# A two-layer graph network on one core: the first layer's symmetric products by half, its matrix engine in program order, part of its weighting on GpSimd

## The chip, the cores and the metric

The kernel runs on one core of a Trainium2 chip. A core has TensorE (PE, which multiplies matrices and also transposes blocks, writing to PSUM), VectorE (DVE), ScalarE (ACT), GpSimd (POOL, which can't read PSUM) and the DMA queues that SP, ACT and POOL issue. Each engine works through its own queue in order and waits at semaphores. The metric is the device time of one execution in microseconds (us).

## What is computed

There are 16 batches (graphs) of 1024 nodes with 128 features, and a 1024 x 1024 weighted adjacency per batch whose pattern of non-zeros is symmetric while its weights are not. The first layer normalizes x and runs three convolutions one after the other:

```python
def _adapt_conv(h, edge_weight, W, b, is_last):
    h = h @ W + b
    nh = h / jnp.maximum(norm, EPS)          # norm of each row of h
    cos = jnp.einsum('bij,bkj->bik', nh, nh)
    ew = edge_weight * cos
    h = jnp.einsum('bpq,bqc->bpc', ew, h)
    # relu, except after the last
```

The matrix `cos` is symmetric; `edge_weight` (the adjacency) is not. The result is added to x. The second layer first thins out the adjacency's pattern ("dilation"): row by row, a row with more than ten neighbours loses about two of them, at even ranks, and what is removed in a row is removed in the mirrored column too, which later rows see. Then three graph convolutions on the thinned adjacency with batch normalization follow, a linear map, and a second residual sum. The dilation depends on the adjacency alone, not on the first layer.

## The kernel before

N = 1024 is cut into `NCH` = 8 blocks of P = 128. The program has three stages: the first layer together with the dilation; then, after a branch, the first graph convolution with the thinned adjacency (`masked`, `Sums`); then the other two (line 811 sums them) and the output.

**First layer** (lines 196 to 367). `order` lists the 48 convolutions, the layers of two batches alternating. `adjT_tile` (196) loads a column strip of the adjacency (`nat`), transposes its eight blocks on PE, copies them on ACT (line 145) to a tile of its own, and has POOL write it out for later stages (205). For a convolution, `features` (223) multiplies with the weights, `turned` (245) makes the transposed features `nhT`, `scaled` (251) the normalized ones `hS` (squares on ACT, one product on POOL, line 259). Eight steps q follow. `products(q)` (267) multiplies block row q of `nhT` with all of `nhT`, two pieces of 512 columns (line 274, PSUM tile `pg`), and DVE weights each piece straight from PSUM with the transposed adjacency into `ew` (line 277). `sums(q)` (280) adds `hS[q]` times `ew` into the PSUM tile `po` (line 286), `LAG` = 2 steps later. After the eighth, ACT copies `po` out (line 291). `residual` (296) transposes the result back and adds x, `next_layer` (312) normalizes for the second layer; both write out by POOL's queue. All f32 matmuls run as two passes each.

**Dilation** (lines 387 to 539). For each of eight row blocks k and each half of the batches (`BH` = 8 of them), `dilate` loads the adjacency rows (`an`) and, for k > 0, earlier decisions (`kl`, from DRAM, written by line 538), makes the 0/1 pattern on ACT (412, 413), transposes the earlier decisions on PE (`pk`, 421) and merges them on DVE (422). PE and ACT make a table T (437 to 448). Then `ROUNDS[k]` rounds of a fixed-point iteration follow: DVE compares (line 479, eight instructions of 128 columns in f16), PE counts removals (`pc`, 487), DVE subtracts (503). In the end, for every batch, DVE scans the pattern (530, 1024 columns), ACT takes a distance (531), DVE forms the keep mask (534, 537), and POOL writes it out (538).

**What sets the order.** Both parts are Python generators. `dilation()` yields weights; after each, `step0` (546) runs first-layer units until the first layer has got `SPREAD` = 0.96 times the same share of its units as the dilation has of its weights (lines 541 to 556). A unit is one step q with whatever is attached to it. The tile framework then schedules each engine's instructions by its own estimate of readiness, so an engine's order need not be the program's. PSUM tiles of the first layer come from `ps_sm`, `ps_g` and `ps_o`, those of the dilation from `ps_k`, two buffers each (`ps_o` one).

**Hand-over** (lines 559 to 590, 672). PE sums a vector of mishaps (`pf`), the value is loaded into registers, and a branch runs the dilation again in an exact form if it isn't zero. Then SP loads 17 pieces of weights, and `fetch(0)` loads the first batch's keep mask (`kb`) and normalized features for the second stage.

Of the kernel before, what the change touches and what calls it, by code (L numbers as in the profile page):

```python
# [16 lines left out]
P = 128  # L17
# [15 lines left out]
EW = 4  # L33

LAG = 2

LAG1 = 2

# [5 lines left out]
def tile_adj_preln_d2(  # L44
# [94 lines left out]
    def transposed(psum_pool, dst, src, nm, func=AF.Copy):  # L139

        for h in range(NHALF):
            pt = psum_pool.tile([P, CPH, P], F32, tag="sm", name=f"pt_{nm}_{h}")
            for c in range(CPH):
                nc.tensor.transpose(pt[:, c, :], src[:, h * CPH + c, :], ident)  # L144
            nc.scalar.activation(dst[:, h * CPH : (h + 1) * CPH, :], pt, func)  # L145


    with ExitStack() as actx:
# [3 lines left out]
        ps_g = actx.enter_context(tc.tile_pool(name="a_g", bufs=2, space=PSUM))  # L152
        ps_o = actx.enter_context(tc.tile_pool(name="a_o", bufs=1, space=PSUM))
        ps_k = actx.enter_context(tc.tile_pool(name="a_k", bufs=2, space=PSUM))
# [3 lines left out]
        for i in range(3):  # L158
            nc.sync.dma_start(w0[:, i, :], W[i])
            nc.sync.dma_start(b0[:, i, :], bW[i].partition_broadcast(P))  # L160
# [22 lines left out]
        nc.sync.dma_start(mi, nodemask.rearrange("b (c p) -> (b c) p", p=P))  # L183
# [12 lines left out]
        def adjT_tile(b, q):  # L196

            nat = pool2.tile([P, NCH, P], F32, tag="nat", name=f"nat_{b}_{q}")
# [3 lines left out]
            t = pool1.tile([P, NCH, P], F32, tag="adjT", bufs=2 * NCH + 1, name=f"adjT_{b}_{q}")  # L202
            transposed(ps_sm, t, nat, f"a{b}_{q}")
            t = t.rearrange("p c q -> p (c q)")
            nc.gpsimd.dma_start(adjT_d[b][q], t)
            return t

        class Batch:


            def __init__(self, b):
                self.b, self.l, self.aT, self.rn = b, 0, [], None

            def load(self):
                b = self.b
                xb = pool2.tile([P, NCH, D], F32, tag="xb", name=f"xb_{b}")
                nc.sync.dma_start(xb, x[b].rearrange("(c p) d -> p c d", p=P))
                h = pool2.tile([P, NCH, D], F32, tag="tt", name=f"h_{b}")
                layernorm_relu(pool2, h, xb, f"l0_{b}")
                self.hT = pool2.tile([P, NCH, P], F32, tag="hT", name=f"hT_{b}")  # L220
                transposed(ps_sm, self.hT, h, f"h{b}")

            def features(self, h):

                nm, l, rn = f"{self.b}_{self.l}", self.l, self.rn
                if h == 0:
                    self.hN = pool1.tile([P, NCH, D], F32, tag="hN", bufs=2, name=f"hN_{nm}")
                hc = slice(h * CPH, (h + 1) * CPH)
                pw = ps_sm.tile([P, CPH, P], F32, tag="sm", name=f"pw_{nm}_{h}")
                for c in range(CPH):  # L230
                    nc.tensor.matmul(
# [13 lines left out]
            def turned(self):  # L245

                nhT = pool1.tile([P, NCH, P], F32, tag="nhT", bufs=2, name=f"nhT_{self.b}_{self.l}")
                transposed(ps_sm, nhT, self.hN, f"n{self.b}_{self.l}")
# [18 lines left out]
            def products(self, q):  # L267

                nm = f"{self.b}_{self.l}_{q}"
                ew = pool2.tile([P, N], F32, tag="ew", bufs=EW, name=f"ew_{nm}")  # L270
                for h in range(NHALF):
                    pg = ps_g.tile([P, HALF], F32, tag="pg", name=f"pg_{nm}_{h}")
                    hs = slice(h * HALF, (h + 1) * HALF)
                    nc.tensor.matmul(  # L274
                        pg, lhsT=self.nhT[:, q * P : (q + 1) * P], rhs=self.nhT[:, hs], start=True, stop=True
                    )
                    nc.vector.tensor_tensor(ew[:, hs], pg, self.aT[q][:, hs], ALU.mult)  # L277
                return ew

            def sums(self, q, ew):  # L280
                nm = f"{self.b}_{self.l}"
                if q == 0:
                    self.po = ps_o.tile([P, N], F32, tag="po", name=f"po_{nm}")
                for h in range(NHALF):
# [603 lines left out]
```

## Time and profile before

| | |
|---|---|
| three runs | 3245.83, 3253.26, 3254.17 us; median 3253.26 |
| the profiled execution's own time | 3257.55 us |
| its span, first to last instruction | 3255.8 us, mean granted TensorE clock 0.963 |
| busy over the span | PE 2909.8 (89%), weight loads 2013.4 (62%), DVE 2131.6 (65%), ACT 1138.5 (35%), POOL 439.1 (13%) |
| first layer and dilation | 0 to about 1936 us |
| hand-over | about 1936 to 1977 us |
| second layer, first convolution | about 1977 to 2500 us |
| second layer, the rest | about 2500 to 3256 us |

How to read the profile: a row of a group names the line, the engine, the operation, what it writes and reads, the shape and the count; after the bar stand the busy time and the mean length of one instruction in ns, and after the second bar the time that the engine sat idle just before such instructions and what ended it. A timeline row has the start in us, the length, and the number of instructions merged into it. Matmuls are pipelined: the length of one overlaps the next, so the distance of starts tells the rate. A row that ends in "q" (SPq) belongs to an engine's sequencer, such as an issue of a DMA.

### The profile page before, as it was taken

The page shows a single profiled execution, that of the slowest core. Times are in us where ns is not written, and L with a number is a line of the kernel's source. Part 1 is how long each engine was busy: PE and PEld are TensorE (multiplying, and loading weights), DVE is VectorE, ACT ScalarE, POOL GpSimd, SP SyncE. Part 2 cuts the span into 40 slices and gives each one's busy share as a digit, 9 for nine tenths or more (in the row PEclk, how much of TensorE's full clock was granted, in tenths as well). Part 3 has the DMA queues.
Part 4 walks back from the last instruction along what each step waited for, and adds up shares of the span by engine and source line. Part 5 has one row for each costly group of instructions (what it writes and reads, how often), then busy time and mean ns, then how long its engine had stood idle before and what let it go on. Part 6 is the DMA issues. An engine that isn't in the chain of part 4 may idle for free. (4 is left out here: it accounts for less than half of the span.)

```text
span 3255.8 us, 45268 instructions
## 1 busy us (share of the span) xinstructions
PE 2909.8 (89%) x16547; PEld 2013.4 (62%) x16547; DVE 2131.6 (65%) x5319; ACT 1138.5 (35%) x2709; POOL 439.1 (13%) x539
## 2 busy tenths in 40 slices
PE   5999999899999999999999986888877999999996
PEld 4444445445454444445455436787766999889996
DVE  4668758868868768867877945666665333355555
ACT  6536445445345344345244211111111233222223
POOL 1111112012112012011111101111111000100000
PEclk9999999999999999999999998898988999999998
DMA  8337246246255264366175009999996666656663
GB/s 267 134 119 234 81 145 205 85 154 197 77 181 181 75 210 159 92 221 196 40 226 169 26 25 331 340 346 345 345 334 215 206 201 201 200 193 225 226 216 123
DMA packets 423271, 614.65 MB, mean 189 GB/s; under 512 B 80512, under 2 KB 296064, under 8 KB 423040
## 3 DMA queue, kind: packets, MB, share of 16 engines
q1 hardware_dynamic: 338048, 410.32, 39.7%
q0 software_dynamic: 51712, 184.58, 14.7%
q10 hardware_dynamic: 33280, 16.78, 1.8%
q8 instruction: 132, 2.16, 0.3%
q14 instruction: 99, 0.81, 0.1%
HBM read 418.65 MB, written 192.94 MB: 188 GB/s over the span
## 5 line engine op out<-in xcount | busy, mean ns | idle before, releaser
L274 PE MATMUL pg<-nhT 128*128 128x512 f32 x1536 | 771.9, 614 | 58.0 <-DVE ew L277 56.2
L286 PE MATMUL po<-ew,hS 128*128 128x512 f32 x1536 | 742.9, 601 | 3.1 <-POOL hS L259 2.6
L277 DVE TENSOR_TENSOR ew<-pg,adjT 128x512 f32<-128x512 f32 x768 | 516.4, 686 | 214.6 <-PE pg L274 205.8
L286 PEld LDWEIGHTS po<-ew,hS 128*128 128x128 f32 x1536 | 284.5, 192 | 318.2 <-issue 315.2
L811 PE MATMUL agg<-hw,aT 128*128 128x128 f32 x4096 | 472.0, 275 | 0.0
L811 PEld LDWEIGHTS agg<-hw,aT 128*128 128x128 f32 x4096 | 466.7, 192 | 4.0
L274 PEld LDWEIGHTS pg<-nhT 128*128 128x128 f32 x1536 | 263.8, 193 | 281.0 <-issue 151.1
L530 DVE TENSOR_TENSOR_SCAN rank<-patt 128x1024 f16<-128x1024 f16 x128 | 300.2, 2348 | 0.1
L710 PE MATMUL agg<-hw,aT 128*128 128x129 f32 x2048 | 263.5, 287 | 12.1 <-DVE aT L687 11.8
L710 PEld LDWEIGHTS agg<-hw,aT 128*128 128x128 f32 x2048 | 254.0, 202 | 19.4 <-DVE aT L687 12.5
L531 ACT ACTIVATE rank<-rank,fin 128x1024 f16<-128x1024 f16 x128 | 146.9, 1147 | 303.6 <-DVE rank L530 258.4
L687 DVE SCALAR_TENSOR_TENSOR aT<-raw,both 128x1024 f32<-128x1024 f32 x128 | 161.1, 1260 | 131.2 <-DMA raw<-adjT 129.5
L619 PE MATMUL pw<-wrx,hT 128*128 128x256 f32 x768 | 193.9, 404 | 10.4 <-ACT hT L764 9.7
L145 ACT ACTIVATE adjT<-pt_a 128x512 f32<-128x512 f32 x256 | 141.4, 591 | 164.7 <-PE pt_a L144 156.0
L621 DVE TENSOR_TENSOR own<-pw,bs 128x256 f32<-128x256 f32 x192 | 78.8, 422 | 182.3 <-ACT hw L620 182.3
L637 POOL TENSOR_TENSOR o<-o,rn_s 128x1024 f32<-128x1024 f32 x48 | 91.1, 1899 | 658.6 <-DVE rn_s L636 620.2
L620 ACT ACTIVATE hw<-pw 128x256 f32<-128x256 f32 x192 | 73.7, 384 | 301.8 <-PE pw L619 276.7
L619 PEld LDWEIGHTS pw<-wrx,hT 128*128 128x128 f32 x768 | 151.9, 204 | 34.9 <-ACT hT L764 10.5
L144 PEld LDWEIGHTS pt_a<-ident,nat 128*128 128x128 f32 x1024 | 123.2, 146 | 80.3 <-issue 48.1
L257 ACT ACTIVATE hS<-hN 128x128 f32<-128x128 f32 x384 | 113.7, 297 | 168.1 <-DVE hN L241 96.5
L144 PE MATMUL pt_a<-ident,nat 128*128 128x128 f32 x1024 | 149.6, 287 | 20.7 <-DMA nat<-in_adj_dram 10.5
L259 POOL TENSOR_TENSOR hS<-hN,rn 128x1024 f32<-128x1024 f32 x48 | 106.4, 2217 | 440.0 <-DVE rn L128 196.4
(154 smaller groups left out, 3550.9 us busy)
## 6 DMA issues: line engine op xcount, KB each, us to landing
aT<-adT SPq DMA_DIRECT2D x256, 512.0 KB, 4.3
an<-in_adj_dram SPq DMA_DIRECT2D x128, 512.0 KB, 4.8
nat<-in_adj_dram SPq DMA_DIRECT2D x128, 512.0 KB, 4.9
adjT<-adjT POOLq DMA_DIRECT2D x128, 512.0 KB, 5.1
raw<-adjT SPq DMA_DIRECT2D x128, 512.0 KB, 6.5
adT<-aT POOLq DMA_DIRECT2D x128, 512.0 KB, 7.1
keep<-kp POOLq DMA_DIRECT2D x128, 256.0 KB, 2.3
kb<-keep SPq DMA_DIRECT2D x128, 256.0 KB, 10.6
```

The costliest lines, as they stand in the source:

```text
L144: nc.tensor.transpose(pt[:, c, :], src[:, h * CPH + c, :], ident)
L145: nc.scalar.activation(dst[:, h * CPH : (h + 1) * CPH, :], pt, func)
L257: nc.scalar.activation(hS[:, c, :], self.hN[:, c, :], AF.Square, accum_out=ss[:, c : c + 1])
L274: nc.tensor.matmul(pg, lhsT=self.nhT[:, q * P : (q + 1) * P], rhs=self.nhT[:, hs], start=True, stop=True)
L277: nc.vector.tensor_tensor(ew[:, hs], pg, self.aT[q][:, hs], ALU.mult)
L286: nc.tensor.matmul(self.po[:, hs], lhsT=self.hS[:, q, :], rhs=ew[:, hs], start=q == 0, stop=q == NCH - 1)
L530: nc.vector.tensor_tensor_scan(rank, pt[:, 1 : N + 1], pt[:, 2:], 0.0, ALU.add, ALU.add)
L531: nc.scalar.activation(rank, rank, AF.Abs, bias=shift[:, i : i + 1])
L619: nc.tensor.matmul(pw[:, i, :], lhsT=hT[:, 2 * h + i, :], rhs=wrx[:, l, :], start=True, stop=True)
L687: nc.vector.scalar_tensor_tensor(aT, raw, 0.0, both, ALU.max, ALU.mult)
L710: nc.tensor.matmul(self.place(c), lhsT=aT[:, c * P : (c + 1) * P], rhs=self.hw[:, j, :], start=False, stop=j == NCH - 1 and (c % GA == GA ...
L811: nc.tensor.matmul(agg[:, c, :], lhsT=aT[:, c * P : (c + 1) * P], rhs=hw[:, j, :], start=False, stop=j == NCH - 1 and c % CPH == CPH - 1,)
```

## The change

`products` computes only the block columns from q to the end (36 of 64 blocks per convolution). ACT copies them from PSUM to an SBUF tile `g`; POOL multiplies `g` with the adjacency row into the first part of `ew`. `turn`, one step later, transposes the blocks of `g` right of the diagonal on PE into a PSUM tile of a new pool `ps_t`, and DVE weights these into the second part of `ew`. `sums`, three steps later (`LAG` = 3), adds the first part in pieces inside a PSUM bank; `sums_back` adds the mirrored blocks one by one into column block q of `po`, each with its own `hS` block as weights. The steps go through the block rows as `SEQ` says, a long row and a short one in turn. All matmuls and transposes of this stage are held in program order by `tc.keep_in_program_order`.

Beside that: the transposed adjacencies of two batches lie in one tile `adjA`, and strips (`adj_piece`) are loaded ahead and transposed at fixed places (`pieces`); x is kept in a tile of the batch (`fetch`), the first layer's norm is split off (`norm`, `enter`). The yields of the first layer carry PE's estimated time (`COLS` per block of a matmul, `TURN` per transpose), those of the dilation have other weights and more places. `rows` loads the dilation's rows one batch ahead. The dilation's PSUM tiles come from `ps_sm`; `ps_k` is gone. ACT copies `pe` to SBUF before DVE subtracts it. Counting on PE (`removed`) stands after the yield that follows DVE's comparisons. The first layer's weights are loaded by ACT's queue, the second layer's 17 pieces by POOL's, after `fetch(0)`. The last batch's `residual` and `next_layer` stand after the branch.

```diff
-EW = 4
-LAG = 2
+SEQ = (0, 7, 1, 6, 2, 5, 3, 4)
+LAG = 3
...
+COLS, TURN = 0.215, 0.109
...
+        def matmul(*args, **kwargs):
+            tc.keep_in_program_order(nc.tensor.matmul(*args, **kwargs))
...
+            def products(self, s):
+                q = SEQ[s]
+                row = NCH - q
...
+                most = max(NCH - c for c in SEQ[s % 2 :: 2])
+                g = pool1.tile([P, most, P], F32, tag=f"g{s % 2}", name=f"g_{nm}")
+                for c in range(0, row, CPH):
+                    n = min(CPH, row - c)
+                    pg = ps_g.tile([P, CPH, P], F32, tag="pg", name=f"pg_{nm}_{c}")
+                    matmul(
+                        pg[:, :n, :].rearrange("p c q -> p (c q)"),
+                        lhsT=self.nhT[:, q * P : (q + 1) * P],
+                        rhs=self.nhT[:, (q + c) * P : (q + c + n) * P],
+                        start=True,
+                        stop=True,
                     )
-                    nc.vector.tensor_tensor(ew[:, hs], pg, self.aT[q][:, hs], ALU.mult)
...
+                    nc.scalar.activation(g[:, c : c + n, :], pg[:, :n, :], AF.Copy)
+                nc.gpsimd.tensor_tensor(
+                    ew[:, :row, :],
+                    g[:, :row, :],
+                    self.aT[:, q, q * P :].rearrange("p (c q) -> p c q", q=P),
+                    ALU.mult,
+                )
+                return ew, g
...
+            def turn(self, s, ew, g):
...
+                for c in range(1, row, CPH):
+                    n = min(CPH, row - c)
+                    pt = ps_t.tile([P, CPH, P], F32, tag="gt", name=f"gt_{self.b}_{self.l}_{q}_{c}")
+                    for i in range(n):
+                        transpose(pt[:, i, :], g[:, c + i, :], ident)
+                    at = row + c - 1
+                    nc.vector.tensor_tensor(
+                        ew[:, at : at + n, :],
+                        pt[:, :n, :],
+                        self.aT[:, q + c : q + c + n, q * P : (q + 1) * P],
+                        ALU.mult,
                     )
...
+            def sums_back(self, s, ew):
...
+                for n in range(1, NCH - q):
+                    matmul(
+                        self.po[:, q * P : (q + 1) * P],
+                        lhsT=self.hS[:, q + n, :],
+                        rhs=ew[:, NCH - 1 - q + n, :],
...
+                    if now:
+                        behind.append((now, s, *now.products(s)))
+                        yield (NCH - q) * COLS
+                    late = None
+                    if len(behind) > LAG or not now:
+                        late, s_, ew, _ = behind.pop(0)
+                        late.sums(s_, ew)
+                        yield (NCH - SEQ[s_]) * COLS
+                    if s > 0 and now or s == 0 and i:
+                        b_, *of = behind[-2 if now else -1]
+                        if now or s == 0:
+                            b_.turn(*of)
+                            yield (NCH - 1 - SEQ[of[0]]) * TURN
+                    if late:
+                        late.sums_back(s_, ew)
+                        yield (NCH - 1 - SEQ[s_]) * COLS
...
-                yield 0.75
+                yield 3.0
...
-                    yield 0.1
+                    yield 2.5
...
-                    yield 0.1
+                    yield 1.0
...
-                    pc = removals(x, f"{nk}_{r}")
-                    yield 1.5
+                    removals(x, f"{nk}_{r}")
+                    yield 5.0
+                    pc = removed(f"{nk}_{r}")
                     x = pool2.tile([P, BH], F32, tag="x", name=f"x_{nk}_{r}")
                     nc.vector.tensor_tensor(x, x0, pc, ALU.subtract)
+                    yield 1.0
...
-                yield 2.5
+                yield 3.5
...
-                yield 1.3
+                yield 2.0
...
+        blocks = NCH * (NCH + 1) // 2
+        conv = (blocks + NCH * NCH + NCH) * COLS + (blocks - NCH + NCH + NCH) * TURN
+        total0 = 3 * B * conv
+        total = 2 * (NCH * (BH * 8.5 + 3.5 * (BH // GT) + 4.0) + sum(ROUNDS) * 6.0)
...
+        batches[-1].residual()
+        batches[-1].next_layer()
```

## The prediction

> **What bounds the kernel now.** I read the busy times by stage first, then the start times on TensorE (PE), then its waits, then GpSimd (POOL) against VectorE (DVE). The first layer and the dilation fill 0 to 1936 us; a hand-over follows to 1977, and two stages that this change leaves alone. Columns: busy us of PE, weight loads, DVE, ACT, POOL, each with its count, then granted clock, DMA share, GB/s.
>
> ```profile
> 60.00:1865.00 1805.00, 1668.28 (x6866) 871.52 (x6865) 1385.92 (x3510) 802.10 (x2098) 263.24 (x322) 0.99 0.46 147
> 1865.00:1936.00 71.00, 70.76 (x189) 32.88 (x187) 32.88 (x75) 9.70 (x32) 6.08 (x5) 1.00 0.06 19
> ```
>
> PE is 92% busy in the long part, yet a busy PE row holds modelled tails, so I count passes by start times. An f32 matmul is two passes.
>
> ```profile
> 1020.34 1.88 PE L274 MATMUL pg<-nhT 128*128 128x512 f32 x4
> 1022.06 1.88 PE L286 MATMUL po<-ew,hS 128*128 128x512 f32 x4
> 1023.77 1.04 PE L144 MATMUL pt_h<-ident,h 128*128 128x128 f32 x8
> 1024.65 1.88 PE L274 MATMUL pg<-nhT 128*128 128x512 f32 x4
> ```
>
> Four passes of 512 columns take 1.72 us from start to start (0.429 each); eight f32 transposes take 0.88 (0.109 each). Blocks of 128 columns with their own weights are shown by a later stage, 128 passes in 14.29 us, 0.112 each:
>
> ```profile
> 2527.71 14.46 PE L811 MATMUL agg<-hw,aT 128*128 128x128 f32 x128
> 2542.00 3.19 PE L619 MATMUL pw<-wrx,hT 128*128 128x256 f32 x14
> ```
>
> So the first stage issues: products 1536 x 0.429 = 659; sums 659; features 768 x 0.112 = 86; f32 transposes 1664 x 0.109 = 181; the dilation's f16 work (1088 at 0.056, 624 narrow ones at 0.028 from start to start) 78. Sum 1663 of 1936 us. The other **273 us are gaps**: 48 in the first 100 us, the rest in stalls. Where they lie shows in one unit of the dilation (128 rows, eight batches), rows and rounds first, then its keep phase (scan, rank, keep):
>
> ```profile
> 1041.00:1119.00 78.00, 75.73 (x318) 38.05 (x317) 54.25 (x178) 31.14 (x95) 7.19 (x5) 1.00 0.29 86
> 1119.00:1161.00 42.00, 37.39 (x103) 16.92 (x102) 41.21 (x71) 13.73 (x28) 7.81 (x8) 1.00 0.12 44
> ```
>
> In the keep phase DVE is busy 41.2 of 42 us: there DVE is the bound and PE waits. Summed over the 16 units by start times, keep phases last 721 us with 118 of the gaps and rounds 268 us with 47, so 165 lie in DVE-bound phases and 108 elsewhere. The groups that matter:
>
> ```profile
> L274 PE MATMUL pg<-nhT 128*128 128x512 f32 x1536 | 771.9, 614 | 58.0 <-DVE ew L277 56.2
> ...
> L277 DVE TENSOR_TENSOR ew<-pg,adjT 128x512 f32<-128x512 f32 x768 | 516.4, 686 | 214.6 <-PE pg L274 205.8
> ...
> L259 POOL TENSOR_TENSOR hS<-hN,rn 128x1024 f32<-128x1024 f32 x48 | 106.4, 2217 | 440.0 <-DVE rn L128 196.4
> ```
>
> PE's largest wait is for the weighting on DVE (56 us), and DVE waits longest for PE's products (206 us).
>
> **The change, part by part.** There are 48 convolutions (16 batches x 3 layers), "conv" below.
>
> *PE.* Of 64 product blocks 36 stay: 36 x 2 x 0.1075 = 7.7 us a conv instead of 13.7, 288 us less in all. The 28 mirrored blocks are transposed: 28 x 0.109 x 48 = +147. Their sums go from 512-wide passes to 128-wide ones: 28 x 2 x (0.112 - 0.107) x 48 = +12. PE issues 1663 - 288 + 147 + 12 = 1534 us, **129 less**, all of it on the engine that sets the end of this stage.
>
> *DVE.* Line 277 had 768 instructions, 0.600 us apart when back to back: 461 us. The mirrored blocks are 10 instructions a conv; at the same slope (0.133 a block and 0.067 an instruction) 4.4 x 48 = 211. DVE loses 250 us. Bare, that pays the 165 us of gaps in the DVE-bound phases, but see POOL.
>
> *ACT.* It gains 12 copies from PSUM a conv, nine 512-column pieces' worth at the 0.485 of line 145's starts, 4.5 x 48 = 216 us, and 16 copies of `pe` at line 135's 1.06, 17 us. Its start-to-start load goes from 810 to 1043 of some 1800 us, hidden beside PE. If that cover fails (ACT waits for a scan with copies queued behind it), PE's two `pg` buffers fill, and the price is the length of the wait; the ACT waits for scans sum to 206 us between 200 and 1800.
>
> *POOL.* 36 blocks a conv are 4.5 pieces of 1024. Line 259 has the same shape with one input broadcast: 1.89 us undisturbed, so 8.5 x 48 = 408 us more; its longest, 3.93, would make 849. POOL's 280 us of now leave room for either, and `LAG` 3, three steps of 28/8 us, gives some ten us before a sum needs the piece. I take 1.89, the undisturbed row, as POOL's own work. The Trainium skill (GPSIMD Engine Reference, "Elementwise — side-by-side cycle accounting") has 4497 ns for a two-input f32 instruction of 2048 elements; an estimate from it is 2.25 a piece and 486 us, which no run here shows for two full inputs. On POOL's queue the pieces stand behind the keep and adjacency writes, which wait for DVE and ACT (63 waits for line 537 of 5.1 us each between 200 and 1800); that is under the ten us, so I take 0, though a piece later than that stops PE at its sum, and ACT's copy two steps on, as `g` has one buffer for even and one for odd steps: the price is then the excess, 128 x up to 5 us. But the two engines shut each other out:
>
> ```profile
> 1235.38 2.29 DVE L530 TENSOR_TENSOR_SCAN rank<-patt 128x1024 f16<-128x1024 f16 x1
> ...
> 1235.74 3.61 POOL L259 TENSOR_TENSOR hS<-hN,rn 128x1024 f32<-128x1024 f32 x1
> ...
> 1238.16 3.34 DVE L530 TENSOR_TENSOR_SCAN rank<-patt 128x1024 f16<-128x1024 f16 x1
> ```
>
> ```profile
> 719.19 1.89 POOL L259 TENSOR_TENSOR hS<-hN,rn 128x1024 f32<-128x1024 f32 x1 [0.66 <-DVE th L384]
> 719.22 1.89 DVE L473 SCALAR_TENSOR_TENSOR at<-th 128x8 f32<-128x8 f32 x1
> ```
>
> POOL started during a scan and took 3.61 instead of 1.89; the next scan then took 3.34 instead of 2.29. An 8-column DVE instruction that started just after POOL's ended with it, 1.89 us (its usual mean is 0.24). Line 277, with one input in PSUM, kept its 0.68 us beside POOL.
>
> The Trainium skill (SBUF — State Buffer, "Who interferes with whom") says why: a DVE instruction with both inputs in SBUF, or in a two-port mode, and a GpSimd instruction that reads SBUF exclude each other for the whole instruction, whoever starts first. The rows agree with it, and it speaks against this change: by the rule at its worst, no POOL piece beside any DVE instruction, the sum comes to the full-exclusion rival's 3257; by line 277's undisturbed rows alone it comes to 3015.
>
> So the DVE-bound phases, per row of the keep phase: after the change the program places 5.5 of its weights there, each 0.96 x 1345/1636 = 0.79 us of PE (its own totals), so 4.34 + 0.06 of dilation = 4.4 us PE. DVE has scan 2.26, line 537 0.61, line 534 0.49, line 527 0.13 (mean distances of starts), 3.5 us; the first layer's part is 8.8 us (4.4 mirrored blocks, 4.4 lines 241, 307, 111 and their like, from starts) in a conv's 28 us of PE, 0.31 x 4.34 = 1.35; together 4.85. POOL has 0.37 x 4.34 = 1.6 (8.5 and line 259's 1.9, of 28). If POOL costs DVE nothing, 4.85 - 4.4 = 0.45 x 128 = 58 us of gaps; if all of it does, 2.05 x 128 = 263, and 37 more in 62 rounds (5.5 against 4.9 us). I take the middle, (58 + 300)/2 = 179, about the 165 of now, because of a keep row's 4.85 us of DVE some 70% is excluding kind and the rest can run beside POOL. **The gaps stay as they are.**
>
> *Order.* PE is pinned to program order. The waiting groups (112 `pk`, 32 `pdt`, 32 `pT`, 62 `pc`, 16 `pe`, 254 in all) hold back whatever of the first layer stands behind them. Now the gaps ahead of these groups sum to 79 us. The yields put 2 to 4 us of PE work before each, against for instance 3.5 us of DVE in a round, so I take no change; bounds: -29 (the `kl` waits, with rows now fetched one ahead) and +302 (254 waits at the 1.5 us of a `kl` wait now, less the 79).
>
> *SP.* Rows, `kl` and adjacency pieces are issued one ahead at the same sizes; the DMAs are 46% busy in this stage, which hides them.
>
> *Start.* The first adjacency tiles no longer share the SP queue with the dilation's rows, but these come later: between -25 and +20, taken as 0.
>
> *Hand-over.* SP issued 17 weight DMAs before the first `kb`:
>
> ```profile
> 1948.05 0.36 SPq L584 DMA_DIRECT2D wrx<-in_L_gnn_Wr_dram  x1
> ...
> 1957.53 10.42 SPq L672 DMA_DIRECT2D kb<-keep  x8
> ```
>
> They go to POOL's queue behind `kb`, which gives up to 9.5 us; against it the last batch's residual and norm move behind the branch and may hold memory that `kb` takes. Between -11 and 0; I take -6.
>
> Sum against the profiled execution (3257.55, span 3255.8; the median of the runs is 3253.26, 4 lower): 3257.55 - 129 - 6 = 3122, by the median 3118. I say **3120**.
>
> **Rivals.**
>
> *Relieved DVE* (gaps shrink): POOL's pieces fall beside PSUM work. DVE-bound gaps fall from 165 to 58: 3122 - 107 = 3015. For it: 250 us less DVE, waits of POOL itself have slack. Against: 70% of a keep row excludes.
>
> *Full exclusion:* those gaps become 300: 3122 + 135 = 3257, no change. For it, the five rows above; against, line 277's kind runs beside POOL.
>
> *Program order* (slower): 254 pinned waits at 1.0 to 1.5 us each, 254 to 381 less the 79 of now: 3297 to 3424, some 3360. For it: 14 `pc` waits now average 0.94 us and 20 `kl` waits 1.5, DVE is full in the phases that feed `pc`, and both `sm` buffers now serve dilation and first layer. Against: the spacing above. It decides from (129 + 6 + 79)/254 = 0.84 us a wait.
>
> **How the numbers follow.** Forecast 0.40 (3070 to 3170); relieved DVE 0.25; full exclusion 0.17 (3180 to 3270, of it 0.09 faster, 0.06 same, 0.02 slower); program order 0.18. About 0.3% (10 us) can be told from no change. Faster 0.40 + 0.25 + 0.09 = 0.74, same 0.06, slower 0.20. The range 2990 to 3290 leaves out a little of relieved DVE and nearly all of program order.
>
> **What would show it.** Products at 36/64 of 1536 passes, 1344 transposes of `g`; PE's issue near 1534 with gaps near 273; scans of 3 us and more by the dozen if exclusion holds; PE's waits led by DVE's weighting of the mirrored blocks (DVE-bound) or by `pc`, `pk`, `pT` (program order); `kb` issued within some 3 us of the branch. Wrong if PE waits for ACT's copies or for POOL's pieces by over 100 us, which I priced at nothing.

## The result, and the profile after

The changed kernel is **slower**: 3386.98 us, the median of four runs (3383.34 to 3400.34), against 3253.72 for the kernel before on the same chip. The ratio is 1.042, with a 95% interval of 1.039 to 1.046. The profiled execution took 3385.13 us, its span 3383.3. The forecast was 3120, and the measured time lies 97 us above the upper end of the range. Line numbers from here on are those of the kernel that is spoken of.

The page of the changed kernel, its head and its costliest groups:

```profile
span 3383.3 us, 53792 instructions
...
PE 2877.8 (85%) x19811; PEld 2352.0 (70%) x19811; DVE 2105.8 (62%) x5319; ACT 1442.5 (43%) x3445; POOL 1052.7 (31%) x940
...
L161 PE MATMUL po<-ew,hS 128*128 128x128 f32 (+3 forms) x3840 | 832.0, 353 | 68.5 <-ACT hTo L368 63.9
L312 POOL TENSOR_TENSOR ew<-g,adjA 128x1024 f32<-128x1024 f32 (+7 forms) x384 | 612.3, 1598 | 563.9 <-issue 262.5
...
L161 PE MATMUL pg<-nhT 128*128 128x512 f32 (+3 forms) x1152 | 474.7, 523 | 23.9 <-ACT g L311 23.6
```

POOL's busy time more than doubles: its new products (line 312) take 612 us, where 408 were forecast. DVE, which was to lose 250 us, lost 26 (2131.6 to 2105.8). Its weighting did shrink, from line 277's 516 us to line 330's 239. But without POOL's products the same DVE instructions are busy 1911.8 us (e2 below), so 194 us of the 2105.8 are lengthening beside POOL. And PE's largest wait is no longer for DVE's weighting but for ACT's copy `hTo` out of `po`.

Another part is work that nobody uses. The statistics of the first normalization, before and after:

```profile
L111 DVE BATCH_NORM_STATS2 ln_st_l<-xb 128x6 f32<-128x128 f32 x128 | 32.4, 268 | 17.2 <-DMA xb<-in_x_dram 17.2
```

```profile
L114 DVE BATCH_NORM_STATS2 ln_st_l<-xb 128x6 f32<-128x128 f32 x256 | 64.4, 265 | 29.8 <-DMA xb<-in_x_dram 29.8
```

The changed kernel normalizes x of every batch twice. `then.norm()` stands at step 0 and asks whether the batch is still in its first layer (`then.l == 0`); ahead of the batch's second convolution that still holds, because with `LAG` = 3 `l` is raised only at step 2. The second result is never read. By the instructions added, it keeps DVE busy for some 56 us and ACT for 62 (line 122 goes from 128 to 256 instructions on `xb`). It is in every run made from the changed kernel, and no run leaves it out, so what it costs in time is not known.

The stretches of the stage (busy us of PE, weight loads, DVE, ACT, POOL with counts, granted clock, DMA share, GB/s):

```profile
60.00:1865.00 1805.00, 1511.47 (x9289) 1101.19 (x9288) 1300.61 (x3356) 1030.30 (x2617) 770.30 (x630) 0.93 0.46 146
1865.00:2020.00 155.00, 138.41 (x754) 99.65 (x752) 78.78 (x174) 72.72 (x192) 72.91 (x57) 0.96 0.19 64
```

PE was 92% busy in the long part before and is 84% now. No other engine is near full over the whole of it, so the bound has to be looked for by phase. One unit of the dilation, first its rows and rounds, then its keep phase:

```profile
1075.00:1169.00 94.00, 81.32 (x512) 59.12 (x512) 60.10 (x233) 57.36 (x164) 35.36 (x29) 0.93 0.53 168
1169.00:1207.00 38.00, 28.26 (x131) 19.97 (x129) 37.93 (x45) 14.94 (x27) 18.54 (x14) 0.87 0.12 45
```

In the keep phase DVE is full, as before (37.9 of 38 us), but PE has only 28.3 us of work there, against 37.4 of 42. The table sums this over all units from PE's start times. A gap is what a distance of starts has over the usual one for that shape; "issue" is the length of the stage, to PE's last sum, less the gaps. All in us, good to some 5 us; the prediction's 1663 and 273 for the kernel before came from counting instructions. "No pinning" and "no POOL" are the experiments below.

| kernel | end of the stage | PE issue | gaps | rows | rounds, and to the scan | keep phase | after the last |
|---|---|---|---|---|---|---|---|
| before | 1936 | 1670 | 266 | 94 | 53 | 118 | 0 |
| after | 2072 | 1545 | 527 | 154 | 92 | 272 | 9 |
| no pinning (e1) | 1978 | 1544 | 434 | 122 | 64 | 245 | 3 |
| no POOL, unweighted (e2) | 1944 | 1545 | 399 | 151 | 57 | 182 | 9 |
| neither, unweighted (e7) | 1832 | 1545 | 287 | 108 | 25 | 151 | 3 |
| DVE weights, pinned (e3) | 1976 | 1550 | 426 | 137 | 70 | 208 | 12 |
| DVE weights, no pinning (e8) | 1870 | 1545 | 325 | 115 | 40 | 164 | 5 |

PE's issue fell by 125 us, as forecast. The gaps rose by 261. The stage is 136 us longer and what follows is 8.5 shorter (from the end of the last `hTo`: 1319.0 before, 1310.4 after); together that is the difference of the spans, 127.5. Of the 261 us, 154 lie in the keep phases.

What PE waits for in the first 2060 us (us in total, times, longest):

```profile
PE po L161 <- ACT hTo L368: 63.9, 30, 6.7
PE gt L164 <- DVE ew L330: 49.7, 27, 8.2
PE pt_h L164 <- DVE x L382: 31.3, 14, 8.5
PE pg L161 <- ACT g L311: 21.4, 13, 2.9
PE pk L164 <- DMA kl<-keep: 18.0, 5, 4.5
PE pw L161 <- ACT adjA L148: 16.5, 24, 4.2
...
PE po L161 <- POOL ew L312: 4.5, 6, 0.8
```

Five of the first six belong to the first layer itself; only `pk` is the dilation's. PE's matmuls hardly wait for POOL by name. What POOL does to DVE, and what a held order does to PE, a keep phase shows. GpSimd, VectorE, ScalarE and TensorE, from the timeline of the same 12 us:

```profile
1182.90 3.67 POOL L312 TENSOR_TENSOR ew<-g,adjA 128x896 f32<-128x896 f32 x1
```

```profile
1182.42 2.28 DVE L670 TENSOR_TENSOR_SCAN rank<-patt 128x1024 f16<-128x1024 f16 x1
1184.62 2.50 DVE L677 TENSOR_TENSOR kp<-kp,patt 128x1024 f16<-128x1024 f16 x1
1187.04 2.28 DVE L670 TENSOR_TENSOR_SCAN rank<-patt 128x1024 f16<-128x1024 f16 x1
```

```profile
1181.55 0.96 ACT L311 ACTIVATE g<-pg 128x512 f32<-128x512 f32 x2
1184.80 1.15 ACT L671 ACTIVATE rank<-rank,fin 128x1024 f16<-128x1024 f16 x1 [2.29 <-DVE rank L670]
1185.85 1.00 ACT L368 ACTIVATE hTo<-po 128x1024 f32<-128x1024 f32 x1
```

```profile
1181.59 1.69 PE L161 MATMUL po<-ew,hS 128*128 128x512 f32 x8
1183.12 0.60 PE L161 MATMUL pg<-nhT 128*128 128x256 f32 x2
1187.00 3.36 PE L161 MATMUL po<-ew,hS 128*128 128x512 f32 x4 [3.29 <-ACT hTo L368]
```

Two things are to be seen, and they are separate. POOL's product and DVE's two instructions take turns: the product, begun during a scan, lasts 3.67 us (the shortest of this shape lasts 2.07), and the comparison of line 677, elsewhere in this phase 0.68 us, lasts 2.50 and ends 0.55 after the product does. And ACT stands idle for 2.29 us at line 671, which waits for the scan of 1182.42; the copy `hTo`, whose sums ended at 1183.28, is behind it in ACT's queue and starts at 1185.85. PE's next sum needs the single `po` buffer, and in a held order nothing behind it may go ahead: 3.29 us of PE are lost. This second loss is not POOL's work: the scan has its usual length here, 2.28 us, and in e2, without POOL's products, PE waits as long for `hTo` (61.5 us against 63.9).

The hand-over did not go as forecast. The first `kb` was to be issued within some 3 us of the branch. It takes 4.43 us on SP's queue instead of 10.42, but it is issued 22.6 us after the last `hTo`, where the kernel before needed 20.7: the queue waits for the write-out of the last batch's normalized features, which now stands behind the branch.

```profile
SPq L815 <- DMA h<-h: 17.3, 1, 17.3
```

```profile
2095.47 4.43 SPq L815 DMA_DIRECT2D kb<-keep  x8
```

The 8.5 us less after the last `hTo` cannot be credited to it either: runs that keep the hand-over of before need 1311.8 (e9), 1313.0 (e10) and 1304.1 us (e13) there.

### The profile page after: what moved, and what is told of

Same layout as the page of the kernel before. It is cut to its first block, busy times and chain, and to the rows that moved or that the text cites. A ratio compares the mean times of both kernels' runs of the same rounds, so it can differ in the third digit from the quotient of the medians.

```text
span 3383.3 us, 53792 instructions
## 1 busy us (share of the span) xinstructions
PE 2877.8 (85%) x19811; PEld 2352.0 (70%) x19811; DVE 2105.8 (62%) x5319; ACT 1442.5 (43%) x3445; POOL 1052.7 (31%) x940
## 5 line engine op out<-in xcount | busy, mean ns | idle before, releaser
L161 PE MATMUL po<-ew,hS 128*128 128x128 f32 (+3 forms) x3840 | 832.0, 353 | 68.5 <-ACT hTo L368 63.9
L312 POOL TENSOR_TENSOR ew<-g,adjA 128x1024 f32<-128x1024 f32 (+7 forms) x384 | 612.3, 1598 | 563.9 <-issue 262.5
L161 PEld LDWEIGHTS po<-ew,hS 128*128 128x128 f32 x3840 | 550.5, 199 | 212.1 <-issue 134.2
L161 PE MATMUL pg<-nhT 128*128 128x512 f32 (+3 forms) x1152 | 474.7, 523 | 23.9 <-ACT g L311 23.6
L330 DVE TENSOR_TENSOR ew<-gt,adjA 128x512 f32<-128x512 f32 (+1 forms) x480 | 239.1, 522 | 252.8 <-PE gt L164 194.9
L311 ACT ACTIVATE g<-pg 128x512 f32<-128x512 f32 (+2 forms) x576 | 266.6, 484 | 209.1 <-PE pg L161 207.0
L161 PEld LDWEIGHTS pg<-nhT 128*128 128x128 f32 x1152 | 203.3, 205 | 132.2 <-issue 95.7
L164 PEld LDWEIGHTS gt<-ident,g 128*128 128x128 f32 x1344 | 170.0, 147 | 164.0 <-issue 90.4
L853 PEld LDWEIGHTS agg<-hw,aT 128*128 128x128 f32 x2048 | 254.7, 203 | 22.6 <-DVE aT L830 16.5
L164 PE MATMUL gt<-ident,g 128*128 128x128 f32 x1344 | 217.5, 284 | 50.9 <-DVE ew L330 49.7
L671 ACT ACTIVATE rank<-rank,fin 128x1024 f16<-128x1024 f16 x128 | 146.9, 1148 | 258.3 <-DVE rank L670 254.7
L831 POOL DMA_DIRECT2D adT<-aT x128 | 69.3, 541 | 403.3 <-DVE aT L830 259.9
```

Source lines behind the costliest of these rows:

```text
L161: tc.keep_in_program_order(nc.tensor.matmul(*args, **kwargs))
L164: tc.keep_in_program_order(nc.tensor.transpose(*args))
L311: nc.scalar.activation(g[:, c : c + n, :], pg[:, :n, :], AF.Copy)
L312: nc.gpsimd.tensor_tensor(ew[:, :row, :], g[:, :row, :], self.aT[:, q, q * P :].rearrange("p (c q) -> p c q", q=P), ALU.mult,)
L330: nc.vector.tensor_tensor(ew[:, at : at + n, :], pt[:, :n, :], self.aT[:, q + c : q + c + n, q * P : (q + 1) * P], ALU.mult,)
L671: nc.scalar.activation(rank, rank, AF.Abs, bias=shift[:, i : i + 1])
```

## The experiments

**Theories after the result.** A: POOL's weighting costs the time, by shutting out DVE's instructions in the phases where DVE is the bound. B: holding TensorE in program order costs it. C, a rival to both: the new weights of the yields place the wrong amount of first-layer work in the keep phases. Where one run is compared with one run, 10 us (0.3%) is the least that counts; differences from the changed kernel are taken from its profiled execution, 3385.13.

**e1: the order is left to the scheduler.**

```diff
-            tc.keep_in_program_order(nc.tensor.matmul(*args, **kwargs))
+            nc.tensor.matmul(*args, **kwargs)
...
-            tc.keep_in_program_order(nc.tensor.transpose(*args))
+            nc.tensor.transpose(*args)
```

> The changed kernel with its first-stage matmuls and transposes left to the scheduler instead of pinned to program order; all else is as changed. Theory Q (pinned PE waits for first-layer copies and weightings that stand behind the keep phase's work in the queues of ACT and DVE): PE can do other work meanwhile, the gaps of the first stage (538 of 2060 us, 272 of them in keep phases) fall to about the 273 of before, so some 3130 to 3200 us. Theory X (POOL's weighting and DVE's keep-phase instructions exclude each other): the order of PE changes nothing in DVE's time, keep-phase gaps stay above 230, time 3340 to 3400.

Measured 3291.68, between the two ranges: 93 us of the change's loss are B. All phases have smaller gaps (table), the keep phase least in proportion (272 to 245).

**e2: no GpSimd product.** ACT copies `pg` straight to `ew`; the upper half stays unweighted, all else is as in the change.

```diff
-                    nc.scalar.activation(g[:, c : c + n, :], pg[:, :n, :], AF.Copy)
-                nc.gpsimd.tensor_tensor(
-                    ew[:, :row, :],
-                    g[:, :row, :],
-                    self.aT[:, q, q * P :].rearrange("p (c q) -> p c q", q=P),
-                    ALU.mult,
-                )
-                return ew, g
+                    nc.scalar.activation(ew[:, c : c + n, :], pg[:, :n, :], AF.Copy)
+                return ew, ew
```

> The changed kernel without POOL's weighting of the upper half: ACT copies the products straight into the first part of ew, the mirrored blocks are transposed from there, and the upper half stays unweighted (this part of the computation is left out). PE, ACT and DVE do the same instructions as changed. Theory X: without POOL's 612 us of pieces DVE's keep rows shrink (scan 2475 to 2285 ns, keep comparison 943 to 690), keep-phase gaps fall from 272 to about 60 to 120, time 3180 to 3250. Theory Q: the copies still stand behind the distances that wait for scans, gaps fall by under 60, time 3320 to 3370.

Measured 3260.09: 125 us are A. The DVE groups of the keep phase, first with the change (the stage), then in e2:

```profile
L670 DVE TENSOR_TENSOR_SCAN rank<-patt 128x1024 f16<-128x1024 f16 x128 | 315.7, 2475 | 0.1
...
L677 DVE TENSOR_TENSOR kp<-kp,patt 128x1024 f16<-128x1024 f16 x128 | 120.5, 943 | 0.6
```

```profile
L662 DVE TENSOR_TENSOR_SCAN rank<-patt 128x1024 f16<-128x1024 f16 x128 | 290.3, 2277 | 0.1
...
L669 DVE TENSOR_TENSOR kp<-kp,patt 128x1024 f16<-128x1024 f16 x128 | 89.7, 703 | 0.6
```

The same instructions on the same data are 0.20 and 0.24 us shorter without POOL beside them. The keep phases take 584 us instead of 676, and their gaps 182 instead of 272; the rounds' gaps go from 92 to 57. Among PE's waits it is the one for DVE's weighting of the mirrored blocks (49.7 with the change) that shrinks, and not the one for `hTo`:

```profile
PE po L161 <- ACT hTo L360: 61.5, 35, 5.7
...
PE gt L164 <- DVE ew L322: 21.2, 14, 5.3
```

**e3: DVE weights the upper half** from PSUM, as the kernel before did; ACT's copies to `g` stay.

```diff
-                nc.gpsimd.tensor_tensor(
-                    ew[:, :row, :],
-                    g[:, :row, :],
-                    self.aT[:, q, q * P :].rearrange("p (c q) -> p c q", q=P),
-                    ALU.mult,
-                )
+                    nc.vector.tensor_tensor(
+                        ew[:, c : c + n, :],
+                        pg[:, :n, :],
+                        self.aT[:, q, (q + c) * P : (q + c + n) * P].rearrange("p (c q) -> p c q", q=P),
+                        ALU.mult,
+                    )
```

> The changed kernel with the upper half weighted on DVE from PSUM, as before the change, instead of on POOL; ACT still copies for the transposes. DVE gains 576 instructions, about 4608 columns a convolution at 1.04 ns and 12 times 67 ns, 5.6 x 48 = 269 us, POOL loses 612. Theory X: what DVE loses in exclusion (some 100 us of longer scans and comparisons) comes back, so the time is within 3340 to 3400 although DVE has 269 us more. Theory Q: DVE's queue gets longer in keep phases while ACT's waits stay, gaps grow by 100 or more, time 3450 to 3600.

Measured 3296.02, below both ranges. DVE is given 303.5 us of work (busy time of its group of line 312), and the kernel is 89 us *faster*: the same work is cheaper on the engine that is full than on the one that is idle.

**e5: other weights in the keep phase** (theory C), so that the program places less first-layer work there.

```diff
-                yield 3.5
+                yield 1.5
...
-                yield 2.0
+                yield 1.0
...
-        total = 2 * (NCH * (BH * 8.5 + 3.5 * (BH // GT) + 4.0) + sum(ROUNDS) * 6.0)
+        total = 2 * (NCH * (BH * 5.5 + 3.5 * (BH // GT) + 4.0) + sum(ROUNDS) * 6.0)
```

> The changed kernel with lighter weights in the keep phase: 1.5 and 1.0 in place of 3.5 and 2.0 a row (8.5 becomes 5.5 in the total), so that the program places about 2.6 us of PE a keep row instead of 4.3, and more beside the rows and rounds. Theory Q: less first-layer work is pinned behind scans, keep-phase gaps fall to under 200 and rows take up the rest at little cost: 3280 to 3340. Theory X: DVE's keep rows are as long as they were and the same pieces exclude; gaps move with the work but the sum of keep-phase lengths stays near 676 and PE does less in them: 3370 to 3430.

Measured 3393.85, no change (+9): the keep phases last 650 us instead of 676, with the same gaps, 273. Nothing speaks for C, but the edit moved little: PE's issue in the keep phases (their length less their gaps) fell from 404 to 377 us. More work in the keep phases was not tried.

**e6: a third buffer in the pool shared by dilation and first layer**, taken from `ps_t`.

```diff
-        ps_sm = actx.enter_context(tc.tile_pool(name="a_sm", bufs=2, space=PSUM))
+        ps_sm = actx.enter_context(tc.tile_pool(name="a_sm", bufs=3, space=PSUM))
...
-        ps_t = actx.enter_context(tc.tile_pool(name="a_t", bufs=2, space=PSUM))
+        ps_t = actx.enter_context(tc.tile_pool(name="a_t", bufs=1, space=PSUM))
```

> The changed kernel, complete and pinned, with three PSUM buffers instead of two in the pool that the first layer's entry, features, turns and residual share with the dilation, and one instead of two for the transposed blocks. In the changed kernel the pinned PE's groups that wait for a buffer of that pool (pw, pt_n, pt_h, px, pt_a, pk behind ACT or DVE) have some 100 us of gaps that the unpinned kernel has half of. If the shared pool is what pinning costs: those gaps halve, 3320 to 3350, in spite of the single buffer of gt. If pinning costs by whatever is late, not by that pool: 3375 to 3430.

Measured 3520.55, 135 us more. PE's waits in the first 1980 us say why:

```profile
PE gt L164 <- DVE ew L330: 299.1, 150, 6.3
```

The single `gt` buffer costs more than any sharing could give back, so the run tells nothing of the sharing.

**e7: e1 and e2 together** (upper half unweighted).

> The changed kernel without POOL's weighting of the upper half (left out of the computation, as in e2) and without the pinning of PE (as in e1). If exclusion and the order of PE are two separate costs, their gains add: 3385 - 125 - 93 = some 3165 us, and the keep-phase gaps fall below the 118 us of before. If they are one cost seen twice (pinned PE waits for what exclusion makes late), the second brings little: 3220 to 3260.

Measured 3143.49. From the changed kernel that is 242 us; the two parts alone gave 93 and 125, 218 together. The causes are separate: together they bring 24 us more than the parts, so neither is the other seen twice.

**e8: e1 and e3 together**, the whole computation with neither cause.

> The changed kernel, complete, with the upper half weighted on DVE (as in e3) and PE not pinned (as in e1). Separate costs: 3385 - 89 - 93 = some 3200 us, faster than before. One cost seen twice: 3270 to 3300, since DVE is full in the keep phases whoever orders PE.

Measured 3185.06, 70 us under the kernel before in the same session (3255.59).

**e9: POOL's load alone, on the kernel before.** After each step POOL multiplies as many elements as in the change into a tile that nobody reads; the rest is the kernel before.

```diff
+                row = N - q * P
+                spare = pool1.tile([P, N], F32, tag="spare", name=f"spare_{nm}")
+                nc.gpsimd.tensor_tensor(spare[:, :row], self.nhT[:, :row], self.aT[q][:, :row], ALU.mult)
                 return ew
```

> The kernel before, with one idle POOL product of (8 - q) x 128 columns a step (the changed kernel's sizes, 384 instructions, 408 us undisturbed) whose result nobody reads: the exclusion by itself, with no first-layer work waiting for POOL. Exclusion theory: DVE's scans and keep comparisons grow as in the changed kernel, keep phases get longer, +90 to +130 us: 3345 to 3385. If POOL's cost in the changed kernel was its place in the chain (late pieces, its queue), an idle load is free: 3250 to 3265.

Measured 3444.08, +188 us and above the range, for work on which nothing depends. The stage's groups, before and in e9:

```profile
L530 DVE TENSOR_TENSOR_SCAN rank<-patt 128x1024 f16<-128x1024 f16 x128 | 300.2, 2348 | 0.1
...
L537 DVE TENSOR_TENSOR kp<-kp,patt 128x1024 f16<-128x1024 f16 x128 | 87.6, 691 | 0.4
```

```profile
L533 DVE TENSOR_TENSOR_SCAN rank<-patt 128x1024 f16<-128x1024 f16 x128 | 328.2, 2566 | 0.1
...
L540 DVE TENSOR_TENSOR kp<-kp,patt 128x1024 f16<-128x1024 f16 x128 | 122.0, 958 | 0.4
```

The scan takes 2.57 us (before 2.35), the comparison 0.96 (before 0.69), and POOL's 384 products 605.5 us. PE's gaps rise from 266 to 459, most in the keep phases (118 to 217) and the rounds (53 to 134), where DVE's comparison grows from 322 to 410 ns. This is A by itself, unless the products only delay what stands behind them in POOL's queue; the next run fills the same places of that queue.

**e13: the same place, but POOL only writes** (two memsets a step, which read nothing; idle work again).

```diff
+                for part in range(2):
+                    nc.gpsimd.memset(spare[:, :row], float(part))
```

> The kernel before with an idle load on POOL that only writes: two memsets of (8 - q) x 128 columns a step, 768 in all, in place of the idle products of e9. If any POOL instruction shuts DVE out, scans and keep comparisons grow as in e9 in proportion to POOL's busy time, +60 us or more. If only POOL's reading does, the scans (two SBUF inputs) keep their 2285 ns and the time stays within 3250 to 3290; only the one-input comparison (574 ns) may grow.

Measured 3256.78, no change, with POOL busy 449.5 us more, so places in POOL's queue alone cost nothing:

```profile
L281 POOL MEMSET spare<- 128x1024 f32 (+7 forms) x768 | 449.5, 585 | 38.4
...
L541 DVE TENSOR_TENSOR kp<-kp,patt 128x1024 f16<-128x1024 f16 x128 | 87.1, 687 | 0.4
```

The scan is at 2.33 us and the comparison at 0.69, as before. Only the comparisons with one tensor input grew, line 538's from 574 to 655 ns and the rounds' from 322 to 389. So, as far as two runs tell, it is POOL's reading that shuts out DVE's instructions with two inputs in SBUF, and not that POOL is busy (the memsets are shorter too, 0.585 us against 1.577). The Trainium skill (SBUF — State Buffer, "Who interferes with whom") states this split: two SBUF inputs on DVE contend with a GpSimd instruction that reads, not with one that only writes. These two runs agree with it.

**e14 and e15: which order is it?** On e3, TensorE's operations of the first layer alone (e14), or of the dilation alone (e15), are chained in program order; those of the other part are left to the scheduler.

```diff
+        def chain(ins):
+            if last[0] is nc.cur_bb:
+                tc.add_manual_dep(
+                    ins.ins,
+                    last[1],
+                    mybir.DependencyInfo(mybir.DependencyClass.NoSync, mybir.DependencyReason.DATA),
+                    reason="chain",
+                )
+            last[:] = nc.cur_bb, ins.ins.name
...
-            tc.keep_in_program_order(nc.tensor.matmul(*args, **kwargs))
+            chain(nc.tensor.matmul(*args, **kwargs))
```

> As e3 (upper half weighted on DVE, 3296 us pinned; 3185 unpinned in e8), but only the first layer's matmuls and transposes keep their program order among themselves; the dilation's are left to the scheduler and may stand anywhere between them. If pinning costs because the first layer's own operations wait for one another (a residual, features or turn behind DVE or ACT, with independent products behind them): near 3296. If it costs because the dilation's groups are fixed at places among the first layer's: near 3185.

> As e3, but only the dilation's matmuls and transposes keep their program order among themselves, and the first layer's are free. The dilation is a chain of results anyway, so by the first explanation this is near 3185, and by the second (fixed places between the two) near 3185 as well; near 3296 only if the order within the dilation (its batches and transposes) is what costs.

Measured 3287.74 with the first layer chained, which is the held kernel e3 (3296.02), and 3180.07 with the dilation chained, which is the free one e8 (3185.06). PE's waits, first of e14, then of e15:

```profile
PE pg L172 <- DVE ew L323: 77.1, 53, 4.8
PE pt_h L175 <- DVE x L393: 24.1, 14, 4.3
PE pk L564 <- DMA kl<-keep: 20.8, 11, 3.4
PE po L172 <- ACT hTo L379: 18.0, 26, 1.0
PE pt_n L175 <- ACT adjA L148: 15.0, 13, 4.1
```

```profile
PE pg L315 <- DVE ew L323: 73.3, 57, 3.7
PE pk L175 <- DMA kl<-keep: 22.9, 13, 4.3
...
PE pt_h L147 <- DVE x L393: 9.2, 4, 4.2
```

The waits for DVE's weighting and for `kl` are the same in both. What the free order takes away are the first layer's waits on its own chain of results: `pt_h` on the normalized x, `po` on the copy, `pt_n` on an adjacency copy. By gaps ahead of them, `pt_h` falls from 47 to 12 us, `po` from 62 to 37, `pt_n` from 40 to 16 and `pw` from 22 to 8: 98 of the 110 us by which the gaps differ.

**e10: half products alone, on the kernel before.** DVE weights both halves, ACT copies only what is transposed, the scheduler orders PE; no new order of steps, no change in the dilation. The core of the edit:

```diff
+                    if n > skip:
+                        nc.scalar.activation(g[:, c + skip - 1 : c + n - 1, :], pg[:, skip:n, :], AF.Copy)
+                    nc.vector.tensor_tensor(
+                        ew[:, c : c + n, :],
+                        pg[:, :n, :],
+                        self.aT[:, q, (q + c) * P : (q + c + n) * P].rearrange("p (c q) -> p c q", q=P),
+                        ALU.mult,
+                    )
```

> The kernel before with the symmetric products by half and nothing else: 36 of 64 blocks on PE, ACT copies what is transposed, PE transposes 28 blocks one step later, DVE weights both halves from PSUM (as many columns as before, in 22 pieces a convolution instead of 16), sums in place after two steps; the scheduler orders PE, the dilation keeps its PSUM pool and weights, POOL does no weighting. PE issues some 130 us less. If the saving on PE is real and only POOL and the pinning spoiled it: 3130 to 3200. If keep phases are bound by DVE and swallow it (DVE has 6 x 48 x 67 ns = 19 us more): 3220 to 3290.

Measured 3206.34, between its two ranges and 49 us under the kernel before (3255.59). PE issues 1540 us, about as in the change, but its gaps are 350 (before 266): the keep phases grow from 721 to 828 us, with DVE busy for 790 of them (before 705). Of 130 us less issue 84 come back as gaps, 60 of them in the keep phases, where DVE is the bound.

**e11 and e12: a better version.** e11 is e8 with ACT copying only the blocks that are transposed; e12 has `SPREAD` at 1.04 beside that, so that the first layer ends nearer to the dilation.

```diff
-SPREAD = 0.96
+SPREAD = 1.04
...
-                    nc.scalar.activation(g[:, c : c + n, :], pg[:, :n, :], AF.Copy)
+                    new = c == 0
+                    if n > new:
+                        nc.scalar.activation(g[:, c + new : c + n, :], pg[:, new:n, :], AF.Copy)
```

> A complete kernel: the changed one unpinned, with the upper half weighted on DVE from PSUM (e8), and ACT copying only the blocks that are transposed (28 of 36 a convolution, some 40 us less ACT). If ACT's queue is a bound beside DVE's in keep phases: 3150 to 3175. If DVE alone is: 3180 to 3190. Either way faster than both kernels.

> As e11_dve_less_copy with SPREAD 1.04 instead of 0.96: more of the first layer lies beside the dilation and less in the tail, where PE alone is the bound (137 us of e8). If rows and rounds have room on PE (21% and 10% gaps) the tail shrinks at no cost: 20 to 60 us faster than e11. If keep phases are full of DVE and take what is moved: the same within 10 us.

e11 took 3180.68 (ratio to the kernel before 0.977, 0.975 to 0.979), e12 3164.45 (0.972, 0.969 to 0.974): faster than both kernels. The page of e12:

```profile
span 3161.0 us, 53192 instructions
...
PE 2798.1 (89%) x19811; PEld 2298.1 (73%) x19811; DVE 2168.8 (69%) x5895; ACT 1390.2 (44%) x3397; POOL 437.4 (14%) x556
...
L161 PE MATMUL pg<-nhT 128*128 128x512 f32 (+3 forms) x1152 | 468.2, 507 | 75.5 <-DVE ew L314 74.3
```

ACT's lighter copies gave 4 us, which is nothing; `SPREAD` gave 16, a little under the 20 to 60 expected: after the dilation's last mask the first layer runs for 33 us instead of 141. In the keep phases, 723 us, DVE is 98% busy and PE's gaps are 161: there DVE is the bound that is left.

## Why the prediction was wrong, step by step

- **PE, "129 less"**: right. The issue fell from 1670 to 1545 us, 125 less.
- **Hand-over, −6**: the −8.5 that was measured is no proof of it. `kb` was issued later than before, by the very wait that the prediction had set against its saving, and what follows the last `hTo` varies by as much between runs with the same hand-over. The number is luck.
- **POOL, "I take 1.89, the undisturbed row"**: wrong in size. Line 312's shortest instruction of this shape is 2.33 us and the mean 2.54; the row used had one input broadcast. The 384 instructions took 612 us instead of 408; with the shortest of each shape they come to 535. The estimate that it drew from the Trainium skill (GPSIMD Engine Reference, "Elementwise — side-by-side cycle accounting"), 2.25 a piece, was nearer.
- **"I take the middle ... The gaps stay as they are"**: this step failed, though not in what it charged to POOL. That was 179 − 58 = 121 us (107 as it entered the sum, with the 165 of before in place of 179), and POOL's products cost 125 (e2), or 148 with a free order (e1 to e7); the 188 of e9, on the kernel before, shows that the same load can cost more. What failed is the start, 58 us of gaps if POOL costs DVE nothing. e7 is the run for that, without POOL and without the held order: keep phases and rounds still have 151 + 25 = 176 us of gaps, and the time is 3143, 128 over the 3015 that the prediction names for this case. A keep row of e7 took 602/128 = 4.70 us, near the 4.85 of DVE that were forecast, but it held only (602 − 151)/128 = 3.5 us of PE's work, not 4.4. That the changed kernel's keep phases show 272 us, near the 263 of full exclusion, is therefore chance: 151 are there without either cause. Why the relief did not come, no run settles; the second normalization is part of DVE's load there.
- **Order, "I take no change"**: this step failed too, by 93 us (e1), 111 (e3 to e8) or 117 (e2 to e7). It counted only the 254 groups of the dilation. Those behaved as it said: the gaps ahead of them sum to 68 us, 79 before. What stalls is the first layer's own chain (e14 against e15). It had been treated as work that fills waits, never as work that waits.
- **The sum, done again with runs**: 3015, plus 128 of relief that did not come (e7), plus 117 for the order (e2), plus 125 for POOL, is the 3385 of the profiled execution. The forecast of 3120 had 107 for POOL's share and nothing for the other two.
- **ACT's copies at nothing**: the exception that was named with its cover, "ACT waits for a scan with copies queued behind it", came true with another copy. `hTo` stands behind line 671's waits (254.7 us of them in the stage), and PE waits 64 us for `hTo` and 21 for `g`. No single wait reached the 100 us that was to prove the prediction wrong; the loss is spread over many names.
- **The rivals.** Full exclusion met the size of the keep phases' gaps, by chance as said, and lacked the order; 15 scans of 128 took 3 us or more, 6 before. Program order (3297 to 3424) is on the right side and spans the measured time, but for another reason than its own: its 254 groups cost less than before. The two act at once, and the prediction made them exclude each other.

What stays open: why the DVE-bound gaps did not shrink with DVE's load; what the second normalization costs; how much of the order's cost goes through the two `sm` buffers that both parts now share, which e6 could not tell; and whether the many gaps of PE under 120 ns each, 82 us together in the changed kernel and 49 before, are short waits or go with the lower granted clock of the stage (0.93 against 0.99). No run separates these.

## What to carry to other kernels

Before work is moved from a full VectorE to an idle GpSimd, sort what VectorE runs at that time by its inputs: with two in SBUF, the move takes time from VectorE, and TensorE's waits hardly name GpSimd (4.5 us here). A promise that an engine's program order costs nothing has to be checked for every chain in that order, the filler's own too, and for what stands ahead of its producers in the other engines' queues. And a saving on one engine is worth what it saves in the phases which that engine bounds: of the 130 us that halving alone took from PE's issue, 49 reached the time (e10). When a stage is reordered, count each group's instructions before and after: here the first normalization went from 128 to 256 and the second half was of no use.

## What the runs showed of the hardware

A GpSimd product of two full f32 inputs, 128x1024, took at least 2.33 us, and one with a broadcast second input 1.89. GpSimd's products lengthened DVE's two-input comparison from 0.69 to 0.96 us on average and the scan from 2.35 to 2.57, while its memsets left both alone and lengthened only DVE's one-input comparisons, the keep phase's from 0.57 to 0.66 us.
